# Two levels of Strassen for layer 0, and both layers of a two-layer graph network as streams of short pieces in a fixed order

## The chip, the core and the metric

The kernel runs on one core of a Trainium2 chip. The core has TensorE (PE in the profile: matrix products into PSUM; PEld is its weight load), VectorE (DVE), ScalarE (ACT), GpSimd (POOL) and SyncE (SP), which here only issues transfers; "SPq" in a row means the queue of SyncE. Sixteen DMA engines carry the transfers of all queues. The engines run beside each other and wait for each other by semaphores.

The metric is the time of one execution on the device in microseconds (us). The kernel before takes 2339.7 us (median of 3 runs, 2339.16 to 2340.62).

## The reference

There are 128 graphs ("batches") of 128 nodes with 512 features, all fp32. Layer 0 averages over neighbours; layer 1 diffuses with a transition matrix that it computes from its own scores.

```python
# layer 0
agg = einsum('bij,bjf->bif', adj, x) / max(sum(adj, -1), 1e-6)
x   = layernorm(x + relu(concat([x, agg], 2) @ W.T))
# layer 1, K = 3
Xw  = x @ Wv + bv
sj, si = Xw @ aw[:512, 0], Xw @ aw[512:, 0]
e   = leaky_relu(sj[:, None, :] + si[:, :, None] + ab, 0.2)     # a 128 x 128 matrix per batch
T   = adj * exp(e);  T = T / (sum(T, -1) + 1e-12)
H, Xk = 0, x
for k in range(3):
    H = H + Xk @ Wk[k] + bk[k]
    Xk = T @ Xk
out = layernorm(x + relu(H))
```

## The kernel before

The weight products use one level of Strassen: seven products instead of eight. Two batches make the block rows, the two halves of the 512 features the inner blocks, and the two weights of a layer the block columns. ScalarE and VectorE carry partial sums between PSUM banks while TensorE goes on.

```python
def fused_pair(name, lf, rf, mT):            # two batches, 14 matmuls of 512 columns, 2 aggregations
    X, Y, W, Z = (bank(f"{name}{n}") for n in "xywz")
    ...
    product(X, 1, lf, rf, True)
    nc.scalar.copy(Y, X)
    product(Z, 5, lf, rf, True)
    nc.scalar.copy(s5, Z)
    product(X, 6, lf, rf, False)
    nc.vector.tensor_add(W, X, s5)
    ...                                      # products 2, 7, 3 and 4 in the same manner
    nc.tensor.matmul(W, mT[0], u[:, 0], ...) # aggregation with the graph's matrix
    nc.tensor.matmul(Z, mT[1], u[:, 1], ...)
    return W, Z
```

The transition of a group (G = 4 batches, N = 128 nodes) gets its row of scores from TensorE. A transpose of one column, given as if it were 128 equal columns, leaves the row in all 128 partitions of a PSUM bank. Seven banks rotate among the products, and the eighth, of the pool `ps_t`, is for such uses:

```python
def transition(g):
    ...                                      # sc: scores of the group, si: those of the rows, with the constant
    pe = ps_t.tile([P, G, N], FP, name="pe", tag="tr")
    for b in range(G):
        nc.tensor.transpose(pe[:, b, :], sc[:, 0, b : b + 1].to_broadcast([P, P]), ident)
    T = p1.tile([P, G, N], FP, name="T")
    nc.vector.tensor_add(T, pe, si[:, :, None].to_broadcast([P, G, N]))
    nc.vector.scalar_tensor_tensor(T, T, SLOPE, T, ALU.mult, ALU.max)
    nc.scalar.activation(T, T, AF.Exp)
    ...                                      # times adj, rows normalised, blocks swapped by way of DRAM
```

The normalised output y of layer 0 goes to DRAM (`yd`) and comes back in blocks (`yb`), which VectorE transposes into the left factors of layer 1 (`yf`). A loop over pairs of batches calls the parts, with layer 1 three pairs behind:

```python
for t in range(len(steps) + 3):
    ...                                      # loads
    if t < len(steps):
        layer0(g, p)
        y_blocks(g, p)                       # y -> yd (issued by GpSimd), yd -> yb (issued by SyncE)
    ...
    if t >= 3:
        layer1(*steps[t - 3])
    if 1 <= t <= len(steps):
        y_factors(*steps[t - 1])
    if t < len(steps) and p == 1:
        transition(g)
```

Of the kernel before, what the change touches and what calls it, by code (L numbers as in the profile page):

```python
# [15 lines left out]
def kernel(  # L16
# [32 lines left out]

    nc = tc.nc  # L50
    P = 128
# [13 lines left out]
    p3 = ctx.enter_context(tc.tile_pool(name="p3", bufs=3))  # L65
    p5 = ctx.enter_context(tc.tile_pool(name="p5", bufs=5))
    dram = ctx.enter_context(tc.tile_pool(name="dram", bufs=3, space=bass.MemoryType.DRAM))
    small = ctx.enter_context(tc.tile_pool(name="small", bufs=4))
    ps_t = ctx.enter_context(tc.tile_pool(name="ps_t", bufs=1, space=bass.MemoryType.PSUM))
    ps_m = ctx.enter_context(tc.tile_pool(name="ps_m", bufs=7, space=bass.MemoryType.PSUM))  # L70

    def bank(name):
        return ps_m.tile([P, F], FP, name=name, tag="mm")
# [4 lines left out]
    xs, xbs, adjs = {}, {}, {}  # L78
# [8 lines left out]
    def load_x(g, p):  # L87
        b = g * G + 2 * p
        xs[g, p] = p3.tile([P, 2, F], FP, name="xg")
        nc.sync.dma_start(xs[g, p], x[b : b + 2].rearrange("b n f -> n b f"))  # L90

    def load_x_blocks(g, p):
        b = g * G + 2 * p
        xbs[g, p] = p2.tile([P, 2, Q, P], FP, name="xb")
        load_blocks(xbs[g, p], x[b : b + 2])

    def load_adj(g, eng=nc.sync):
        adjs[g] = p3.tile([P, G, N], FP, name="ag")
        eng.dma_start(adjs[g], adj[g * G : (g + 1) * G].rearrange("b i j -> i b j"))

    def load_weight(eng, dst, src, h):

        for q in range(Q):
            eng.dma_start(dst[q * R : (q + 1) * R, h * H : (h + 1) * H],
                          src[q * P + h * H * R : q * P + (h + 1) * H * R].rearrange("(c s) o -> s c o", s=R))


    w0_sb = const.tile([P, 2 * NC, F], FP)
    wk_sb = const.tile([P, K, NC, F], FP)
    wvt_sb = [p5.tile([P, H, F], FP, name=f"wvt{i}", tag="y") for i in range(2)]  # L110
# [4 lines left out]
    w2, w1 = w0_sb[:, NC:, :], w0_sb[:, :NC, :]  # L115
    load_weight(nc.scalar, w2, w0t[F:], 0)
    load_x_blocks(0, 0)
    load_weight(nc.scalar, w1, w0t[:F], 0)
    load_weight(nc.sync, w1, w0t[:F], 1)
    load_weight(nc.scalar, w2, w0t[F:], 1)  # L120
    load_adj(0)
    load_adj(1)
    load_x_blocks(0, 1)
    for i in range(2):
        nc.scalar.dma_start(wvt_sb[i], wvt[i * FH : (i + 1) * FH, :].rearrange("(c p) f -> p c f", p=P))
    load_x(0, 0)
    load_x_blocks(1, 0)

# [4 lines left out]
    ones = const.tile([P, P], FP)  # L133
# [5 lines left out]


    first = [bank(f"first{i}") for i in range(7)]
    for t in first:
        nc.tensor.matmul(t, ident, ident[:, None, :].to_broadcast([P, Q, P]), start=True, stop=True)
    for t in first:
        nc.tensor.matmul(t[:, :1], ident, ident[:, :1], start=False, stop=True, skip_group_check=True)

    def weight_sums(eng, name, b11, b12, b21, b22):

        t = const.tile([P, 3, H, b11.shape[2]], FP, name=name)
        t1, t2, t4 = t[:, 0], t[:, 1], t[:, 2]  # L150
        eng.tensor_sub(t1, b12, b11)
        eng.tensor_sub(t2, b22, t1)
        eng.tensor_sub(b12, b22, b12)
        eng.tensor_sub(t4, b21, t2)
        return [None, b11, b21, b22, t4, t1, t2, b12]

    f0 = weight_sums(nc.vector, "t0", w2[:, :H], w1[:, :H], w2[:, H:], w1[:, H:])


# [5 lines left out]
    def fold_constants():  # L165
        pb = ps_t.tile([P, F], FP, name="pb", tag="tr")
        nc.tensor.matmul(pb, ones[:K], bk_sb, start=True, stop=True)
        nc.scalar.copy(bias, pb)
        nc.vector.tensor_sub(bias[:, FH:], bias[:, FH:], bias[:, :FH])
# [5 lines left out]
        pc = ps_t.tile([P, F], FP, name="pc", tag="tr")  # L175
        nc.tensor.matmul(pc[:, :1], ones, t1, start=True, stop=True)
        nc.vector.tensor_add(cc, pc[:, :1], ab_sb)
        pw = ps_t.tile([P, F], FP, name="pw", tag="tr")
        for c in range(NC):
            nc.tensor.matmul(pw[:2], aw_sb[:, :, c], wvt_sb[c // H][:, c % H, :], start=(c == 0), stop=(c == NC - 1))  # L180
        w2row = p1.tile([2, F], FP, name="w2row", tag="scr")
        nc.scalar.copy(w2row, pw[:2])
        wm = small.tile([2, 1], FP, name="wm")
        nc.vector.tensor_reduce(wm, w2row, AX.X, ALU.add)
        nc.vector.tensor_scalar(wm, wm, 1.0 / F, None, ALU.mult)
        nc.vector.tensor_scalar(w2row, w2row, wm, None, ALU.subtract)
        for t in range(2):
            pr = ps_t.tile([P, F], FP, name="pr", tag="tr")
            nc.tensor.matmul(pr, ident[:2, t : t + 1].to_broadcast([2, P]), w2row, start=True, stop=True)  # L189
            nc.scalar.copy(wrow[:, t], pr)  # L190


    def left_factors(pool, name, src):

        t = pool.tile([P, 7, H, P], FP, name=name)
        a11, a12, a21, a22, s1, s2, s4 = (t[:, i] for i in range(7))
        for i in range(2):
            nc.vector.transpose(t[:, 2 * i : 2 * i + 2].rearrange("p a h (j r) -> p j (a h) r", r=R),  # L198
                                src[:, i].rearrange("p j (c s) -> p j c s", s=R))
        nc.vector.tensor_add(s1, a21, a22)  # L200
        nc.vector.tensor_sub(a21, a11, a21)
        nc.gpsimd.tensor_sub(s2, s1, a11)  # L202
        nc.gpsimd.tensor_sub(s4, a12, s2)
        return [None, a11, a12, s4, a22, s1, s2, a21]

    def product(dst, i, lf, rf, start):
        for c in range(H):
            nc.tensor.matmul(dst, lf[i][:, c, :], rf[i][:, c, :], start=(start and c == 0),  # L208
                             stop=(c == H - 1), skip_group_check=True)

    def fused_pair(name, lf, rf, mT):

        X, Y, W, Z = (bank(f"{name}{n}") for n in "xywz")
        s5 = p2.tile([P, F], FP, name="s5")
        u = p2.tile([P, 2, F], FP, name="u")
        product(X, 1, lf, rf, True)
        nc.scalar.copy(Y, X)
        product(Z, 5, lf, rf, True)
        nc.scalar.copy(s5, Z)
        product(X, 6, lf, rf, False)  # L220
        nc.vector.tensor_add(W, X, s5)  # L221
        product(Y, 2, lf, rf, False)
        nc.scalar.copy(u[:, 0], Y)
        product(X, 7, lf, rf, False)
        nc.vector.tensor_add(Z, X, s5)  # L225
        product(W, 3, lf, rf, False)
        product(X, 4, lf, rf, False)
        nc.scalar.copy(u[:, 1], X)
        nc.tensor.matmul(W, mT[0], u[:, 0], start=False, stop=True, skip_group_check=True)  # L229
        nc.tensor.matmul(Z, mT[1], u[:, 1], start=False, stop=True, skip_group_check=True)  # L230
        return W, Z

    def statistics(mv, t):
        st = small.tile([P, 6], FP, name="st")
        nc.vector.bn_stats(st, t)  # L235
        nc.vector.bn_aggr(mv, st)  # L236

    def layernorm(t, mv, rstd):

        ve = small.tile([P, 2], FP, name="ve")  # L240
        nc.gpsimd.tensor_scalar(ve, mv[:, :, 1], LN_EPS, None, ALU.add)  # L241
        nc.gpsimd.tensor_tensor(rstd, ve, nhalf, ALU.pow)  # L242
        for i in range(2):
            nc.gpsimd.tensor_scalar(t[:, i], t[:, i], mv[:, i, 0:1], rstd[:, i : i + 1], ALU.subtract, ALU.mult)  # L244

    def swap_blocks(name, src):

        d = dram.tile([G, P, N], FP, name=f"{name}d")
        nc.sync.dma_start(d.rearrange("b i j -> i b j"), src)
        t = p1.tile([P, G, Q, R], FP, name=f"{name}b")  # L250
        load_blocks(t, d)
        return t

    xfs, ans, aTs, ys, ybs, yfs, scs, Ts, TTs = {}, {}, {}, {}, {}, {}, {}, {}, {}

    def x_factors(g, p):
        xfs[g, p] = left_factors(p2, "xf", xbs.pop((g, p)))

    def degree_norm(g):
        deg = small.tile([P, G], FP, name="deg")  # L260
        nc.vector.tensor_reduce(deg, adjs[g], AX.X, ALU.add)
        nc.vector.tensor_scalar(deg, deg, DEG_EPS, None, ALU.max)
        rdeg = small.tile([P, G], FP, name="rdeg")
        nc.vector.reciprocal(rdeg, deg)
        an = p1.tile([P, G, N], FP, name="an")
        nc.vector.tensor_mul(an, adjs[g], rdeg[:, :, None].to_broadcast([P, G, N]))
        ans[g] = swap_blocks("an", an)

    def a_transpose(g):
        aTs[g] = p2.tile([P, G, N], FP, name="aT")  # L270
        nc.vector.transpose(aTs[g].rearrange("p g n -> p (g n)"), ans.pop(g).rearrange("p g j r -> p (g j r)"))

    def layer0(g, p):

        ys[g, p] = p5.tile([P, 2, F], FP, name="y")
        if p == 0:
            scs[g] = p2.tile([P, 3, G], FP, name="sc")
        hs = fused_pair("h", xfs.pop((g, p)), f0, [aTs[g][:, 2 * p + i, :] for i in range(2)])
# [152 lines left out]
```

## Time and profile before

| | value | where it is read |
|---|---|---|
| time | 2339.7 us | median of 3 runs |
| profiled span | 2335.1 us, mean granted clock 0.994 | the profile's head |

The main lines, and what they say of a group of four batches, are in the prediction below. This row of the table of instruction groups (line, engine, operation, output and inputs, shape, count; then busy us and mean ns; then the idle time of the engine before it and its releaser) is the broadcast of the scores:

```profile
L311 PE MATMUL pe<-ident,ss 128*128 128x128 f32 x128 | 19.7, 278 | 11.6 <-DVE ss L306 11.6
```

TensorE is busy with it for 19.7 us in the whole run. The 11.6 us of waiting are the start's gap of which the prediction speaks. This row of the list of transfers (output and input, queue, number of issues, size of each, and at the end the median us from issue to landing) is the way back of y:

```profile
yb<-yd SPq DMA_DIRECT2D x256, 128.0 KB, 2.8
```

### The profile page before, as it was taken

How to read it: one execution, taken by the hardware profiler on the slowest of the kernel's cores; microseconds unless marked ns; L12 is line 12 of the kernel's file. 1: busy time of each engine (PE TensorE's matmuls, PEld its weight loads, DVE VectorE, ACT ScalarE, POOL GpSimd, SP SyncE). 2: the span in 40 equal slices, each digit the busy share in tenths (PEclk: the TensorE clock that was granted, in tenths of full speed). 3: DMA queues.
4: the chain of work that ended last, by engine and by line, in shares of the span. 5: the costliest groups of instructions: out<-in, count | busy, mean ns of one | idle time of the engine just before them, and what ended most of it. 6: DMA issues, size and time to landing. Idle time of an engine off the chain costs nothing.

```text
span 2335.1 us, 19605 instructions
## 1 busy us (share of the span) xinstructions
PE 2303.7 (99%) x6316; PEld 1174.9 (50%) x6316; DVE 1263.3 (54%) x2732; ACT 435.8 (19%) x805; POOL 1030.3 (44%) x929
## 2 busy tenths in 40 slices
PE   9799999999999999999999999999999999999997
PEld 3355455455455455554554554555545545545554
DVE  5865555555654655654556555556545555554442
ACT  1111212112112112111121121121111111211211
POOL 3744444534534444435345344444353454454433
PEclk9899999999999999999999999999999999999999
DMA  9543332333323333333333333343233333332210
GB/s 211 136 127 86 106 91 84 92 88 104 94 83 95 95 86 111 86 86 92 88 102 94 85 93 95 86 113 94 78 90 93 97 94 85 94 93 63 63 45 27
DMA packets 363974, 217.33 MB, mean 93 GB/s; under 512 B 148573, under 2 KB 328797, under 8 KB 363872
## 3 DMA queue, kind: packets, MB, share of 16 engines
q1 hardware_dynamic: 342848, 143.19, 24.8%
q0 software_dynamic: 19520, 70.28, 8.2%
q10 hardware_dynamic: 1504, 2.62, 0.5%
q8 instruction: 49, 0.80, 0.1%
q14 instruction: 53, 0.43, 0.1%
HBM read 132.13 MB, written 83.89 MB: 93 GB/s over the span
## 4 chain that ended last, share of the span: by engine, by line
PE 97%; DVE 2%; DMA 1%; POOL 0%; issue 0%; POOLq 0%; ACTq 0%; DVEq 0%
PE vx L208 19%; PE hx L208 19%; PE o L208 16%; PE hw L208 5%; PE vw L208 5%; PE vy L208 5%; PE vz L208 5%; PE hz L208 4%; PE hy L208 4%; PE vz L230 3%; PE hz L230 2%; PE vw L229 2%; PE o L353 2%; PE o L355 2%; PE hw L229 2%; PE pe L311 1%
## 5 line engine op out<-in xcount | busy, mean ns | idle before, releaser
L202 POOL TENSOR_TENSOR yf<-yf 128x256 f32<-128x256 f32 x64 | 51.6, 806 | 906.3 <-DVE mv L236 894.2
L244 POOL TENSOR_SCALAR y<-y,mv,rstd 128x512 f32<-128x512 f32 x128 | 266.3, 2082 | 7.0
L244 POOL TENSOR_SCALAR y<-y,mv,sc 128x512 f32<-128x512 f32 x128 | 266.7, 2087 | 0.6 <-POOL sc L242 0.2
L208 PE MATMUL hx<-w_sb,xf 128*128 128x512 f32 x512 | 254.1, 599 | 2.9 <-DVE hw L221 2.8
L208 PE MATMUL vx<-wk_sb,yf 128*128 128x512 f32 x512 | 242.3, 594 | 0.9 <-DVE vw L221 0.9
L208 PE MATMUL hx<-t,xf 128*128 128x512 f32 x512 | 242.1, 595 | 1.2 <-issue 1.2
L208 PE MATMUL o<-wk_sb,yf 128*128 128x256 f32 x1024 | 242.2, 379 | 0.6 <-DVE o L348 0.6
L208 PE MATMUL vx<-t,yf 128*128 128x512 f32 x512 | 240.6, 592 | 0.0
L208 PEld LDWEIGHTS o<-wk_sb,yf 128*128 128x128 f32 x1024 | 192.1, 190 | 84.0 <-issue 37.8
L346 DVE TENSOR_TENSOR so<-o,bias 128x256 f32<-128x256 f32 x64 | 27.1, 424 | 367.6 <-PE o L208 367.6
L208 PE MATMUL o<-t,yf 128*128 128x256 f32 x768 | 206.9, 379 | 0.0
L208 PEld LDWEIGHTS o<-t,yf 128*128 128x128 f32 x768 | 145.9, 190 | 100.5 <-issue 68.4
L290 DVE SCALAR_TENSOR_TENSOR scr<-y,wrow 128x512 f32<-128x512 f32 x256 | 188.3, 736 | 1.6 <-PE pr L189 0.5
L198 DVE STREAM_TRANSPOSE xf<-xb 128x512 f32<-128x512 f32 x128 | 83.6, 691 | 163.6 <-PE hx L208 154.4
L241 POOL TENSOR_SCALAR ve<-mv 128x2 f32<-128x2 f32 x128 | 38.6, 302 | 299.2 <-DVE mv L236 299.2
L235 DVE BATCH_NORM_STATS2 st<-y 128x6 f32<-128x512 f32 x256 | 167.9, 675 | 2.4
L208 PEld LDWEIGHTS hx<-t,xf 128*128 128x128 f32 x512 | 97.2, 191 | 124.0 <-issue 124.0
L208 PEld LDWEIGHTS vx<-t,yf 128*128 128x128 f32 x512 | 97.3, 190 | 122.4 <-issue 122.0
L208 PEld LDWEIGHTS vx<-wk_sb,yf 128*128 128x128 f32 x512 | 97.3, 191 | 122.0 <-issue 112.2
L208 PEld LDWEIGHTS hx<-w_sb,xf 128*128 128x128 f32 x512 | 95.4, 192 | 75.1 <-issue 57.4
L359 DVE SCALAR_TENSOR_TENSOR y<-o,y 128x512 f32<-128x512 f32 x128 | 85.9, 671 | 71.3 <-PE o L353 71.1
L225 DVE TENSOR_TENSOR vz<-vx,s 128x512 f32<-128x512 f32 x64 | 44.7, 699 | 143.0 <-PE vx L208 142.9
(121 smaller groups left out, 3272.6 us busy)
## 6 DMA issues: line engine op xcount, KB each, us to landing
xb<-in_x_dram SPq DMA_DIRECT2D x256, 128.0 KB, 3.0
xg<-in_x_dram SPq DMA_DIRECT2D x64, 512.0 KB, 4.2
yd<-y POOLq DMA_DIRECT2D x64, 512.0 KB, 3.3
yb<-yd SPq DMA_DIRECT2D x256, 128.0 KB, 2.8
out_dram<-y POOLq DMA_DIRECT2D x64, 512.0 KB, 3.3
ag<-in_adj_dram SPq DMA_DIRECT2D x32, 256.0 KB, 2.8
and<-an SPq DMA_DIRECT2D x32, 256.0 KB, 2.3
anb<-and SPq DMA_DIRECT2D x128, 64.0 KB, 2.7
```

What stands on the lines that cost most here:

```text
L198: nc.vector.transpose(t[:, 2 * i : 2 * i + 2].rearrange("p a h (j r) -> p j (a h) r", r=R), src[:, i].rearrange("p j (c s) -> p j c s", s=R))
L202: nc.gpsimd.tensor_sub(s2, s1, a11)
L208: nc.tensor.matmul(dst, lf[i][:, c, :], rf[i][:, c, :], start=(start and c == 0), stop=(c == H - 1), skip_group_check=True)
L225: nc.vector.tensor_add(Z, X, s5)
L229: nc.tensor.matmul(W, mT[0], u[:, 0], start=False, stop=True, skip_group_check=True)
L230: nc.tensor.matmul(Z, mT[1], u[:, 1], start=False, stop=True, skip_group_check=True)
L235: nc.vector.bn_stats(st, t)
L244: nc.gpsimd.tensor_scalar(t[:, i], t[:, i], mv[:, i, 0:1], rstd[:, i : i + 1], ALU.subtract, ALU.mult)
L290: nc.vector.scalar_tensor_tensor(scr, ys[g, p][:, i, :], 1.0, wrow[:, t, :], ALU.mult, ALU.mult, accum_out=scs[g][:, t, b : b + 1])
L353: nc.tensor.matmul(Q0, tT[0], v1[:, 0], start=False, stop=True, skip_group_check=True)
L355: nc.tensor.matmul(Q1, tT[1], v1[:, 1], start=False, stop=True, skip_group_check=True)
L359: nc.vector.scalar_tensor_tensor(r, q, 0.0, r, ALU.max, ALU.add)
```

## The change

The change wants to save TensorE work. Layer 0's weight product takes two levels of Strassen over four batches: 7 × 7 = 49 products of 256 columns, in place of 2 × 14 of 512 columns. Both layers become generators of short pieces ("streams"). In step t one piece of layer 0 is followed by one of layer 1, which lags 24 steps; a group has 18 steps. All other work stands at numbered places in a table: place 2t comes between the two pieces of step t, and 2t + 1 after both. The order of instructions on every engine is exactly that of the program. The streams take all eight PSUM banks (`bA`, `bB`), every transfer of the steady part is issued by SyncE, and the scores are broadcast by way of DRAM. The diff, cut to its core:

```diff
-    ps_t = ctx.enter_context(tc.tile_pool(name="ps_t", bufs=1, space=bass.MemoryType.PSUM))
-    ps_m = ctx.enter_context(tc.tile_pool(name="ps_m", bufs=7, space=bass.MemoryType.PSUM))
+    psum = ctx.enter_context(tc.tile_pool(name="psum", bufs=1, space=bass.MemoryType.PSUM))
...
+    bA = [psum.tile([P, F], FP, name=f"bA{i}") for i in range(4)]
+    bB = [psum.tile([P, F], FP, name=f"bB{i}") for i in range(4)]
...
+    def outer_pair(i, j, evict):             # two of the seven outer products, side by side in a bank
+        def prod(bank, k, start=False):
+            for h, o in enumerate((i, j)):
+                mm(bA[bank][:, h * FH : (h + 1) * FH], left_of(o)[:, LEFT[k]], right_of(o)[:, RIGHT[k]], start and h == 0)
+        ...
+        prod(0, 6)
+        V.tensor_add(bA[2], bA[0], s5)       # "the L262 add" below
+        prod(1, 2)
+        yield
...
-        pe = ps_t.tile([P, G, N], FP, name="pe", tag="tr")
-        for b in range(G):
-            nc.tensor.transpose(pe[:, b, :], sc[:, 0, b : b + 1].to_broadcast([P, P]), ident)
+        d = dram.tile([G, N], FP, name="scd")
+        nc.sync.dma_start(d.rearrange("b n -> n b"), sc[:, 0, :])
+        Ts[g] = d, si
+
+    def t_load(g):
+        d, si = Ts[g]
+        T = p1.tile([P, G, N], FP, name="T", tag="aT")
+        da = d[:]
+        nc.sync.dma_start(T.rearrange("p g n -> p (g n)"), bass.AP(tensor=da.tensor, offset=da.offset, ap=[[0, P], [1, G * N]]))
...
+    PLACES = {                               # middle groups; the first and the last have tables of their own
+        ... (y_load, 1): 43, ... (t_scores,): 39, (t_load,): 42, (t_exp,): 45, ...
+        (y_turn, 1, 0): 45, (y_turn, 1, 1): 46, ...
...
+    with tc.manual_schedule(engines={ET.PE, ET.DVE, ET.Activation, ET.Pool, ET.SP}):
+        for t in range(NG * NA + LAG + 20):
+            next(a, None)
+            run([(f, *args) for f, args in beside.pop(2 * t, ())])
+            run(late)
+            if t >= LAG:
+                next(b, None)
+            run([(f, *args) for f, args in beside.pop(2 * t + 1, ())])
+            run(later)
```

Here `t_scores` makes the scores and issues their store, `t_load` issues the broadcasting load, `t_exp` adds the two scores and takes the exponential, `y_load` brings y back in blocks, and `y_turn` transposes those.

## The prediction

> **What bounds the kernel now.** I read the page first (busy shares, then the chain that ended last), then the table of stretches for three groups of four batches in the middle of the run, then TensorE's (PE's) timeline, and last the start, engine by engine.
>
> ```profile
> PE 2303.7 (99%) x6316; PEld 1174.9 (50%) x6316; DVE 1263.3 (54%) x2732; ACT 435.8 (19%) x805; POOL 1030.3 (44%) x929
> ...
> PE 97%; DVE 2%; DMA 1%; POOL 0%; issue 0%; POOLq 0%; ACTq 0%; DVEq 0%
> ```
>
> The chain is PE for 97% of the span. A busy PE alone would not prove a limit, because the ends of matmuls are modelled; the chain and the steps between starts do. The stretches, whose columns are length, then busy time of PE, weight loads, VectorE, ScalarE and GpSimd (instructions in brackets), clock, DMA share and GB/s:
>
> ```profile
> 936.00:1007.20 71.20, 71.20 (x198) 36.43 (x197) 38.83 (x85) 13.51 (x25) 31.41 (x28) 1.00 0.34 93
> 1007.20:1078.40 71.20, 71.20 (x198) 36.43 (x197) 38.81 (x85) 13.51 (x25) 31.41 (x28) 1.00 0.33 92
> ```
>
> A group takes 71.2 us, PE never idles and has its full clock, and no other engine passes 55%. The price of a matmul comes from its start-to-start steps in PE's timeline (start, us, then the group; two records make one fp32 matmul):
>
> ```profile
> 1013.14 1.88 PE L208 MATMUL hx<-t,xf 128*128 128x512 f32 x4
> 1014.85 1.88 PE L208 MATMUL hy<-w_sb,xf 128*128 128x512 f32 x4
> ...
> 1006.25 2.75 PE L208 MATMUL o<-wk_sb,yf 128*128 128x256 f32 x12
> 1008.84 1.02 PE L353 MATMUL o<-v,TT 128*128 128x512 f32 x2
> ```
>
> Two matmuls of 512 columns step 1.717 us, so one costs 0.858 us; six of 256 columns step 2.59 us, so one costs 0.432, just half. Columns set the price, and a narrow matmul pays nothing extra. One thing could break that: each matmul brings its own weights.
>
> ```profile
> L208 PEld LDWEIGHTS o<-wk_sb,yf 128*128 128x128 f32 x1024 | 192.1, 190 | 84.0 <-issue 37.8
> L290 DVE SCALAR_TENSOR_TENSOR scr<-y,wrow 128x512 f32<-128x512 f32 x256 | 188.3, 736 | 1.6 <-PE pr L189 0.5
> ```
>
> A load takes 190 ns, a record of 256 columns 216 ns, so it still hides. I use the second row for VectorE's bill below.
>
> **What the Trainium skill says.** "TensorE: Matmul & The Clock Gate", section "Step-by-step: what each phase is for", lets a next weight load run under the current matmul; the step of 0.432 us at 190 ns per load agrees. Its section "What's actually happening" has the clock fall after an idle window of about 3.4 us; here the 11.6 us gap at 74 us leaves a clock of 0.83 over 60 to 100 us, which fits. "SBUF — State Buffer", section "Who interferes with whom", says a VectorE instruction with two SBUF inputs and a GpSimd instruction that reads SBUF shut each other out, while one SBUF input is free of it. The trace agrees in part: a VectorE add of 256 columns at 70.69 us lasted 6.61 us (usually 0.39 to 0.50) while GpSimd made four tensor-tensor operations in a row; but scores at 47.55 us took their usual 0.69 us under a GpSimd normalisation, so I charge the lock to tensor-tensor alone.
>
> **The change, part by part.** (1) TensorE per group of four. Before: layer 0 has 2 pairs x (14 products + 2 aggregations) = 32 units of 512 columns; layer 1 has 2 x (14 + 2 + 7 + 2) = 50; together 82, or 70.4 us. Four broadcasting transposes add 0.45 us (a step of 35.84 against 35.39 us between pairs), and four aggregations that wait for ScalarE's copy step 0.94 instead of 0.86, adding 0.32. Sum 71.2, as measured. After: two levels of Strassen make 49 products of 256 columns = 24.5 units, with 4 aggregations 28.5; layer 1 keeps 50. So 78.5 units = 67.4 us. The transposes are replaced by a DMA broadcast, and a piece of the other layer now stands before an aggregation, so both extras go. Gain: 3.5 x 0.858 + 0.77 = 3.8 us per group, 121 us over 32 groups.
>
> (2) VectorE per group, counted in the new program order and priced from the rows of before: PSUM adds and residuals 21.9 (10 bank adds x 0.696, 22 of 256 x 0.43, 8 residuals x 0.67); statistics 8 x 0.84 = 6.7; scores 8 x (0.736 + 0.08) = 6.5; ten transposes x 0.69 = 6.9; inner sums 8 x 0.42 + 4 x 0.50 = 5.4; outer sums of 896, 896 and 1024 columns at 1.21 us per 1024 = 3.3; degree and transition 6.0. Sum 56.7 us of 67.4: 84%, from 55%. That is the largest new cost. It lies beside PE, but PE waits for those adds in a fixed order.
>
> (3) ScalarE: 13.5 plus smaller copies out of PSUM, about 19 us. GpSimd: 8 normalisations x 2.08 = 16.7, scales 4.7, y sums 3.1, four-wide sums (896, 896, 1024, 1024, 768 columns at 1.9 us per 1024) 8.6: 33 us, 49%, about as before, because its four DMA issues x 0.8 go to SyncE. Transfers stay near a third of DMA's capacity.
>
> (4) The ends. Before, the span less 32 x 71.2 is 57 us: 11 until useful products, constants, the waits up to 100 us, and 13 after the last matmul. After, layer 0 runs 24 pieces alone (32.6 us of PE). VectorE has about 63 us of work ordered before layer 1's first operands: weight sums 8 x 1.2 and 2 x 2.1, x sums, three groups of evictions (about 3.1 each), statistics and scores. It starts near 10 us, so layer 1 begins near 78 us, with 45 us lost by then. The transition's DMA round trips cost perhaps 6 more, layer 1 alone at the end about 3 (an add of 0.43 plus its signal is exposed in each pair), the tail 13: 67 or 68 us, some 11 worse than before.
>
> Sum of the profiled span: 2335 - 121 + 11 = 2225. I add 0.3 us of stall per group, 10 us, as my allowance for 84% VectorE in fixed order: 2235. Timed runs were 4.6 us above the profiled span, so 2240 us.
>
> **The rivals.** First, VectorE becomes the bound. For: 56.7 us, plus lock waits: GpSimd's tensor-tensor work of some 12 us per group covers 18% of it, and if six of VectorE's two-input operations each lost 1.2 us it would reach 64 of 67.4. Gaps of in-order waiting would then show on PE as 2 us or more per group: 2290 to 2310, hardly faster. Against: the adds PE waits for have one SBUF input, and the order puts the score and transition work mostly away from GpSimd's sums; pieces are arranged so that an add runs under other matmuls. Over a piece pair PE has 3.74 us and VectorE 3.15.
>
> Second, PE is never made to wait in the steady part and the start overlaps better than I think: then 2225 less perhaps 10 at the start, plus 4.6: about 2215 to 2220. For: tables of places that differ for the first, middle and last group look fitted with care. Against: the start's VectorE work is in one fixed list.
>
> Third, SyncE's single queue, which now carries all DMA issues in order, blocks behind a store that waits for a normalisation and delays the blocks of x. One delay of 3 us per group would make 2330, and nothing is gained. Against: landing takes 2 to 4 us in the rows of before, and loads are placed several pieces (3.7 us each) ahead of use.
>
> **Range and chances.** No stalls and a better start give the low end, about 2212. Two us of stall per group alone would give 2294; I end the range at 2285, as I hold the ordered lists to be mostly right. Within 2% begins at 2293, which needs the first or third rival nearly whole. Faster 0.91, same 0.08, slower 0.01.
>
> **What would show each step.** In the changed profile a middle group should last 67.4 to 68.5 us with PE above 98% and 256-column matmuls still stepping 0.43; larger steps would say weight loads no longer hide. VectorE should be 55 to 60 us per group; above 62 the lock is at work, and wide sums with long means would name it. The first layer-1 product should stand at 70 to 85 us; earlier or later corrects my start. If the chain shows VectorE or DMA above 8%, a rival has won. The prediction is wrong if the group takes over 69.5 us, or if the ends together cost much other than 68.

## More of the kernel before

Node j's score has to be added along the columns of a matrix whose rows are the nodes i. The kernel gets the scores as one number per partition (node). To use them as a row in every partition, it has to turn them and copy them to all partitions. Both kernels do this once for each group of four batches.

## The result, and the profile after

The changed kernel takes 2543.62 us (median of 4 runs, 2536.62 to 2548.06), beside 2339.43 us for the kernel before (4 runs, 2337.62 to 2340.62). The ratio is 1.0871, with a 95% interval of 1.0845 to 1.0897: slower by 8.7%, and 304 us above the prediction. Ratios here and below are the mean time of one kernel's runs over that of the other's of the same rounds, so they are not quite the ratio of the medians quoted.

The page of the kernel after, its first and fourth parts:

```profile
PE 2288.1 (90%) x7520; PEld 1465.9 (58%) x7520; DVE 1758.7 (69%) x3539; ACT 577.8 (23%) x1286; POOL 1198.1 (47%) x852
...
PE 53%; DVE 21%; DMA 20%; SPq 2%; issue 2%; POOL 1%; DVEq 0%; ACT 0%; POOLq 0%; ACTq 0%
```

PE is now idle for a tenth of the span, and the chain that ended last runs through DMA for a fifth of it, against 1% before. The mean granted clock is 0.947. The groups repeat as regularly as before: the multiplication that makes the scores starts at 84.5 us in the first group and at 2460.7 us in the last, so a group takes (2460.7 − 84.5) / 31 = **76.65 us** on average. The table of stretches (columns as in the prediction), for one middle group and two parts of it:

```profile
1020.00:1096.43 76.43, 69.73 (x232) 44.84 (x232) 53.49 (x108) 17.93 (x40) 35.76 (x25) 0.95 0.36 90
1076.60:1084.90 8.30, 8.30 (x41) 7.29 (x40) 4.76 (x10) 2.48 (x6) 4.55 (x2) 1.00 0.03 1
1084.90:1090.70 5.80, 4.21 (x16) 2.62 (x14) 0.00 (x0) 0.00 (x0) 0.00 (x0) 1.00 0.63 83
```

VectorE has 53.5 us of work in 76.4, so it is not the limit. The second line is odd: for 8.3 us the DMA engines move almost nothing (share 0.03, 1 GB/s). In the third, three engines do nothing at all. SyncE's timeline around those 8.3 us (start, us, then what it issued) says what was under way:

```profile
1076.62 0.36 SPq L451 DMA_DIRECT2D scd<-ss  x1
1084.93 0.33 SPq L459 DMA_DIRECT2D T<-scd  x1
1085.36 1.85 SPq L84 DMA_DIRECT2D yb<-yd  x4
```

The store of the scores is issued at 1076.62 us. The load that reads them back can be issued only when the store has landed, at 1084.9. The blocks of y stand behind that load in the queue, although they have nothing to do with it. Two more lines of the table of stretches divide the time in which the store is under way:

```profile
1077.00:1078.00 1.00, 1.00 (x7) 0.87 (x6) 1.00 (x3) 0.06 (x1) 1.00 (x1) 1.00 0.28 10
1078.00:1084.90 6.90, 6.90 (x34) 6.07 (x33) 3.39 (x8) 2.42 (x6) 3.15 (x2) 1.00 0.00 0
```

The DMA engines are busy within one microsecond (share 0.28); the packet records of the trace put 528 packets of 4 bytes between 1077.51 and 1077.95 us. Then they do nothing for 6.9 us (share 0.00), and only after that does the store count as landed.

VectorE, in its fixed order, takes up the story (square brackets: idle time before, and what ended it):

```profile
1083.98 0.43 DVE L541 TENSOR_TENSOR bB<-bB,os 128x256 f32<-128x256 f32 x1 [2.16 <-PE bB L245]
1090.73 0.69 DVE L465 TENSOR_TENSOR T<-T,si 128x512 f32<-128x512 f32 x1 [6.32 <-DMA T<-scd]
...
1094.30 0.71 DVE L238 STREAM_TRANSPOSE yf<-yb 128x512 f32<-128x512 f32 x1 [2.15 <-DMA yb<-yd]
1094.94 0.67 DVE L262 TENSOR_TENSOR bA<-bA,hs 128x512 f32<-128x512 f32 x1
```

VectorE waits 6.32 us for T, then 2.15 us for the blocks. Only then does it come to the L262 add, whose operands do not depend on either. PE needs that add:

```profile
1088.09 1.02 PE L245 MATMUL bB<-v,TT 128*128 128x512 f32 x2
1095.66 3.47 PE L245 MATMUL bA<-wf,xs 128*128 128x256 f32 x8 [6.54 <-DVE bA L262]
```

PE idles 6.54 us, and then eight records of 256 columns take 3.47 us, which elsewhere take 1.89. From 1095.66 to 1099.13 us the table of stretches gives a granted clock of 0.56. So PE pays once for the wait and once more for a lowered clock. The tables of the whole run, below, show that it is so throughout. The list of transfers, with the median us to landing at the end of each row:

```profile
yb<-yd SPq DMA_DIRECT2D x256, 128.0 KB, 3.3
...
T<-scd SPq DMA_DIRECT2D x32, 256.0 KB, 5.8
...
scd<-ss SPq DMA_DIRECT2D x32, 2.0 KB, 8.1
```

The smallest transfer of the steady part, 2 KB, takes longest to land. It writes "b n -> n b": 512 single numbers, each 4 bytes, one by one, to places of which two in succession are 512 bytes apart. The tables of waits of SyncE's queue and of PE (waiter, what it waited for: total us, times, longest):

```profile
SPq L459 <- DMA scd<-ss: 257.4, 32, 10.0
```

```profile
PE bA L245 <- DVE bA L262: 202.7, 61, 7.1
```

Two stretches of the chain that ended last (start, us, what) show both transfers as its links:

```profile
1076.62 8.29 DMA scd<-ss
1086.76 7.42 DMA yb<-yd
```

### The profile page after: what moved, and what is told of

Same layout as the page of the kernel before. It is cut to its first block, busy times and chain, and to the rows that moved or that the text cites. A ratio compares the mean times of both kernels' runs of the same rounds, so it can differ in the third digit from the quotient of the medians.

```text
span 2534.9 us, 23773 instructions
## 1 busy us (share of the span) xinstructions
PE 2288.1 (90%) x7520; PEld 1465.9 (58%) x7520; DVE 1758.7 (69%) x3539; ACT 577.8 (23%) x1286; POOL 1198.1 (47%) x852
## 4 chain that ended last, share of the span: by engine, by line
PE 53%; DVE 21%; DMA 20%; SPq 2%; issue 2%; POOL 1%; DVEq 0%; ACT 0%; POOLq 0%; ACTq 0%
PE bB L245 34%; PE bA L245 19%; DMA scd<-ss 11%; DVE scr L385 9%; DMA yb<-yd 8%; DVE st L368 3%; SPq L84 2%; DVE bA L262 2%; DVE y L334 2%; DVE bB L510 1%; DVE mv L369 1%; DVE bB L515 1%; DMA wf<-in_w0t_dram 1%; DVE xu L199 1%; DVE xu L197 1%
## 5 line engine op out<-in xcount | busy, mean ns | idle before, releaser
L245 PE MATMUL bB<-wk_sb,yf 128*128 128x512 f32 (+1 forms) x2048 | 741.1, 495 | 6.4 <-DVE yf L238 4.2
L245 PE MATMUL bB<-t,yf 128*128 128x512 f32 (+1 forms) x1536 | 560.7, 488 | 5.9 <-DVE yf L196 5.2
L245 PEld LDWEIGHTS bB<-wk_sb,yf 128*128 128x128 f32 x2048 | 398.5, 195 | 254.2 <-issue 206.3
L245 PE MATMUL bA<-wf,xs 128*128 128x256 f32 x896 | 268.9, 450 | 193.9 <-DVE bA L262 191.6
L245 PEld LDWEIGHTS bB<-t,yf 128*128 128x128 f32 x1536 | 292.5, 191 | 201.3 <-issue 166.4
L245 PE MATMUL bA<-wf,xu 128*128 128x256 f32 x1344 | 346.2, 390 | 22.4 <-DVE bA L262 11.1
L245 PEld LDWEIGHTS bA<-wf,xs 128*128 128x128 f32 x896 | 199.5, 227 | 269.7 <-DVE bA L262 217.8
L245 PEld LDWEIGHTS bA<-wf,xu 128*128 128x128 f32 x1344 | 253.4, 193 | 133.8 <-issue 46.6
L396 POOL TENSOR_SCALAR y<-y,mvo,rstd 128x512 f32<-128x512 f32 x128 | 265.4, 2080 | 7.0
L245 PE MATMUL bA<-wf,xl 128*128 128x256 f32 x896 | 214.5, 379 | 0.2 <-DVE bA L267 0.2
L262 DVE TENSOR_TENSOR bA<-bA,hs 128x512 f32<-128x512 f32 x96 | 65.6, 683 | 62.8 <-PE bA L245 62.8
```

Of the source, the lines that this page charges most:

```text
L245: nc.tensor.matmul(dst, lhsT, rhs, start=start, stop=True, skip_group_check=True)
L262: V.tensor_add(bA[2], bA[0], s5)
L396: S_.tensor_scalar(t, t, mv[:, 0:1], rstd, ALU.subtract, ALU.mult)
```

## The experiments

Theory: the 512-piece store of the scores is the whole cause. It lands late itself, and it holds up the transfers issued after it. VectorE's fixed order passes the delay on to PE, and the lowered clock adds to it. Rivals: VectorE's order alone (the add stands behind waits it does not need), VectorE's load or its exclusion by GpSimd, and the DMA round trip as such, whatever its form.

Each table line below is the median of 4 or 5 runs. "Group" is the average group by the same instruction as above.

| kernel | us | ratio to before | group, us |
|---|---|---|---|
| after | 2543.62 | 1.0871 | 76.65 |
| e1_pe_scores | 2276.54 | 0.9744 | 68.45 |
| e2_yload_first | 2507.57 | 1.0729 | 75.60 |
| e3_late_exp | 2421.71 | 1.0381 | 72.91 |
| e4_filler | 2483.66 | 1.0629 | 75.02 |
| e5_before_dram | 2679.81 | 1.1461 | |
| e6_idle_store | 2453.27 | 1.0487 | 73.95 |
| e7_act_queue | 2402.20 | 1.0274 | |
| e8_start_dve | 2276.70 | 0.9738 | |
| e9_row_store | 2275.56 | 0.9736 | 68.33 |
| e10_idle_store_16b | 2276.93 | 0.9742 | 68.45 |
| e11_idle_store_act | 2368.56 | 1.0134 | 71.24 |
| e12_idle_store_pool | 2283.35 | 0.9767 | 68.51 |

All results were correct. The kernel before took 2336.94 us in the rounds of e1 to e4, 2338.25 in those of e5 to e8, and 2336.58 in those of e9 to e12.

### e1: the scores broadcast by TensorE again

```diff
-        nc.sync.dma_start(d.rearrange("b n -> n b"), sc[:, 0, :])       # and the load of T
+        for b in range(G):                                              # at the place of the load
+            nc.tensor.transpose(bB[3][:, b * N : (b + 1) * N], sc[:, 0, b : b + 1].to_broadcast([P, P]), ident)
-        V.tensor_add(T, T, si[:, :, None].to_broadcast([P, G, N]))
+        V.tensor_add(T, bB[3].rearrange("p (g n) -> p g n", g=G), si[:, :, None].to_broadcast([P, G, N]))
```

At that place of the order bank `bB[3]` holds nothing that is still wanted, so no extra bank is needed.

> The changed kernel with one part undone: the scores go to all partitions by four TensorE transposes into a PSUM bank that is idle then, as in the kernel before, not by a store of 512 single elements and a broadcasting load through DRAM. VectorE and GpSimd keep all their work and their order. Theory 1 (the score's round trip of some 14 us holds SyncE's queue and VectorE's order, and TensorE waits behind them for one add per group): the wait of 6.5 us and the low clock after it go, the transposes cost 0.45 us, so a group falls from 76.4 to about 68 us and the time to 2250 to 2290 us. Rival 2 (VectorE is too full for a fixed order, 52 us in 76): its load is the same, so the group stays above 74 us and the time above 2470. Rival 3 (the narrow pieces themselves cost TensorE more): group above 70 us with no waits and larger steps per matmul.

Measured: 2276.54 us (2275.07 to 2277.82), ratio 0.9744 with an interval of 0.9729 to 0.9758. The change is worth 2.6% once this one part of it is undone. A middle group in the table of stretches, and the store of y in the list of transfers, for which e6 will show another value:

```profile
1011.28:1079.86 68.58, 68.42 (x239) 44.67 (x238) 53.39 (x110) 18.03 (x41) 36.65 (x26) 1.00 0.35 97
```

```profile
yd<-y SPq DMA_DIRECT2D x128, 256.0 KB, 2.7
```

PE is busy for 68.42 of 68.58 us at full clock, and VectorE has nearly the same work as in the kernel after, 53.39 us against 53.49. So the rival "VectorE's load or lock" falls for the steady part. This run does not yet tell the store from the round trip or from the order.

### e2 and e3: another order around the slow store

```diff
 e2, middle groups     -(y_load, 1): 43                      +(y_load, 1): 41
 e3, besides that      -(t_load,): 42  (t_exp,): 45  (t_sums,): 48  (t_norm,): 49
                       +(t_load,): 43  (t_exp,): 49  (t_sums,): 50  (t_norm,): 50
```

> The changed kernel with one place moved for the middle groups: SyncE issues the loads of the y blocks of one pair before the broadcasting load of the scores, so they no longer wait for the score store's landing. VectorE's order is left. If theory 1 holds with both waits (VectorE first for the scores, then for the y blocks), only the second of them goes: the scores still land near 14 us after they were made, the add that TensorE waits for comes some 1.5 us sooner, group about 75 us, time 2490 to 2510 us. If SyncE's queue alone were the cause, the whole wait goes: group 68, time about 2290. If neither matters: 2544.

> As e2_yload_first, and VectorE takes the scores (add, leaky part, then sums and scaling) four places later, behind the transposes of y and the adds that TensorE needs. The slow round trip through DRAM stays as it is. Theory 1 says that only the order makes it costly: no wait of over 2 us for that add, group 68 to 70 us, time 2270 to 2340 us. If the transfers themselves (512 packets of 4 bytes, a load from one row) disturb the other loads, or the later steps of the transition now come too late for the aggregation, a new wait appears and the time stays above 2400.

Measured: 2507.57 us for e2 and 2421.71 us for e3. In e2 the add of T is still placed early, and VectorE still waits 230.9 us for T in 31 groups. In e3, where that add comes late, the wait moves to the blocks of y. VectorE's timeline:

```profile
1045.81 0.71 DVE L238 STREAM_TRANSPOSE yf<-yb 128x512 f32<-128x512 f32 x1 [5.27 <-DMA yb<-yd]
```

The blocks were issued at 1033.24 us, just after the store, and took 10.7 us to land. The order therefore matters (e3 wins back 122 us of the 267 that separate the kernel after from e1), but it does not suffice. A transfer that is independent of the store, and no longer stands behind a wait for it, is late too.

### e4: useless work that keeps TensorE busy

```diff
+    def filler(g):                          # at place 47 of the 30 middle groups
+        for _ in range(7):
+            nc.tensor.matmul(bB[3], ident, ident[:, None, :].to_broadcast([P, Q, P]), start=True, stop=True)
```

> The changed kernel with useless work added: seven matmuls of 512 columns into an idle bank (6.0 us at full clock) in the middle groups, just where TensorE waits for the late add. Results stay right. If the wait of 6.5 us is where theory 1 says and the half clock after it costs what the trace shows (1.6 to 2.9 us per group), the group gets shorter, 76.4 to about 74.5, and the time 2470 to 2510 us. If the clock plays no part: 2544 within 10 us. If TensorE's wait is not there, or the time is limited by TensorE's work: up to 6 us more per group, about 2720.

Measured: 2483.66 us, 60 us less than the kernel after, with seven more matmuls in each of 30 groups. PE's timeline:

```profile
1070.78 6.17 PE L658 MATMUL bB<-ident 128*128 128x512 f32 x14
1076.79 1.89 PE L245 MATMUL bA<-wf,xs 128*128 128x256 f32 x8
```

The filler takes the place of most of the wait (PE still waits 38.3 us in all for the L262 add, against 202.7), and the records after it take 1.89 us instead of 3.47. The mean clock rises from 0.947 to 0.993. So the lowered clock costs about 60 / 30 = 2 us per group on top of the wait. The Trainium skill, "TensorE: Matmul & The Clock Gate", section "What's actually happening", lets full speed return after some 3.4 us of sustained work; 3.4 us at half speed would lose 1.7 us, an estimate from that page which agrees. This agrees with the bill of the kernel after: of its 8.20 us per group over e1, waits for the L262 add explain (202.7 − 9.8) / 32 = 6.0, where 9.8 us is the same wait in e1, and 2.2 us are left.

### e5: the same part alone in the kernel before

```diff
-            nc.tensor.transpose(pe[:, b, :], sc[:, 0, b : b + 1].to_broadcast([P, P]), ident)
+        nc.sync.dma_start(d.rearrange("b n -> n b"), sc[:, 0, :])
+        nc.sync.dma_start(T.rearrange("p g n -> p (g n)"), bass.AP(..., ap=[[0, P], [1, G * N]]))
```

> The kernel before with only the broadcast of the scores changed: store of 512 single elements and broadcasting load on SyncE's queue in place of the four TensorE transposes. One part of the change alone. If the round trip of some 14 us is harmful wherever SyncE and VectorE take things in a fixed order, VectorE waits near 10 us for the scores and TensorE for VectorE's next adds: some 5 us or more per group, time 2480 or above. If only the new kernel's short pieces make it harmful (here a pair step of 35 us lies between, and VectorE has 45% idle): 0.45 us per group less transposing, little waiting, time 2310 to 2350 us. The price of the part alone decides.

Measured: 2679.81 us, ratio 1.1461 (1.1445 to 1.1476). The part costs about 342 us in a kernel with neither Strassen's second level nor the fixed tables. Two rows from its waits of VectorE and of SyncE's queue:

```profile
DVE T L314 <- DMA T<-scd: 368.9, 32, 12.7
```

```profile
SPq L313 <- DMA scd<-ss: 343.2, 32, 11.2
```

The part is harmful by itself, even more so here, where nothing was arranged around it. That the kernel before might hide it, as the other branch of the expectation had it, was wrong.

### e6: a store for which nobody waits

```diff
 e1, and in t_scores:
+        d = dram.tile([G, N], FP, name="scd")
+        nc.sync.dma_start(d.rearrange("b n -> n b"), sc[:, 0, :])      # never read
```

> e1_pe_scores with the store of the 512 score elements put back, its result used by nobody: the transfer without its waits. If only the waits for the scores cost time (SyncE held, VectorE waiting): 2277 us within 10, and the y blocks still land in about 3 us. If the store's small packets keep the blocks of y behind them, as the landing time of 10.7 us in the run with the later exponentials suggests: y blocks land near 10 us, VectorE waits for them, TensorE for VectorE some 2 us and more per group, time 2330 to 2400 us.

Measured: 2453.27 us (2448.10 to 2454.89), above the 2330 to 2400 that I had expected even if the store held up others. A store whose result is never used costs 177 us of the 267. From its list of transfers, its timelines of SyncE and VectorE, and its PE timeline:

```profile
yd<-y SPq DMA_DIRECT2D x128, 256.0 KB, 12.6
...
scd<-ss SPq DMA_DIRECT2D x32, 2.0 KB, 10.2
```

```profile
1043.16 0.36 SPq L451 DMA_DIRECT2D scd<-ss  x1
1043.63 1.92 SPq L84 DMA_DIRECT2D yb<-yd  x4
...
1046.10 1.95 SPq L407 DMA_DIRECT2D yd<-y  x2
```

```profile
1058.20 0.71 DVE L238 STREAM_TRANSPOSE yf<-yb 128x512 f32<-128x512 f32 x1 [5.49 <-DMA yb<-yd]
```

```profile
1059.56 1.99 PE L245 MATMUL bA<-wf,xs 128*128 128x256 f32 x8 [3.46 <-DVE bA L262]
```

The four blocks of y issued right after the store, from 1043.63 us on, come so late that VectorE waits for them until 1058.20, and PE waits for the same L262 add as before. The two stores of y issued next, at 1046.10 us, are held as well: the median of all stores of y is 12.6 us here, against the 2.7 shown for e1. So the store hurts in two ways: by being waited for, and by holding up what is issued after it.

### e7 and e11: the store on ScalarE's queue

```diff
 e7: e3, e11: e6, each with
-        nc.sync.dma_start(d.rearrange("b n -> n b"), sc[:, 0, :])
+        nc.scalar.dma_start(d.rearrange("b n -> n b"), sc[:, 0, :])
```

> e3_late_exp with the score store issued from ScalarE's queue. If the blocks of y were late there because they stood behind the store's 512 packets in the same queue, they now go round them: landing near 3 to 4 us, no wait of VectorE for them, group 69 to 70 us, time 2290 to 2330 us. If it is the sixteen DMA engines that the small packets hold, whichever queue they come from: landing stays near 10 us and the time near 2420.

> As e6_idle_store, with the unused store issued from ScalarE's queue. If transfers behind it in SyncE's own queue were held only by the queue's order: y blocks land in 3 us again, time 2277 to 2300 us. If both queues share what the 512 pieces occupy: landing of the y blocks issued beside it stays at 8 to 12 us and the time within 40 us of 2453.

Measured: 2402.20 us for e7 (e3: 2421.71) and 2368.56 us for e11 (e6: 2453.27; e1: 2276.54). The time of e7 lies between its two branches, and so does that of e11. SyncE's transfers are still held: in e11 the blocks of y take up to 13.6 us to land, and VectorE waits 128.5 us for them, against 172.9 in e6. Their median landing of 2.9 us does not show it, because only one of the two pairs of a group is loaded near the store. By the landing times in the trace (medians of the 30 middle groups, as far as they are recorded), the first of the four blocks is issued 0.13 us before the store in e11 and lands in 4.0 us. In e6 it was issued 0.47 us after the store and took 12.5. The other three, issued after the store in e11 too, take 10.5 to 12.4 us. So a part of the gain can come from the order of issue; whether the queue itself helps is not separated from that.

### e12: the store on GpSimd's queue

The same edit as in e11, with `nc.gpsimd.dma_start`.

> As e6_idle_store, with the unused store issued from GpSimd's queue, which the profile lists as software dynamic. In the first 8 us after the store in the changed kernel the DMA engines were 3% busy, so the pieces seem to wait in front of the engines. If that is in what SyncE's and ScalarE's queues share and GpSimd's does not: y blocks land in 3 us, time 2277 to 2310 us (GpSimd has half its time free for the issue). If the engines or the memory hold the others up: landing near 10 us and time above 2400.

Measured: 2283.35 us (2282.13 to 2284.93), 7 us above e1. It looks as if GpSimd's queue spared the others, but the timelines of SyncE (two lines) and GpSimd give another reason. Under them stand the rows of the store and of the stores of y from the views of transfers:

```profile
1046.73 1.80 SPq L84 DMA_DIRECT2D yb<-yd  x4
...
1049.07 3.07 SPq L407 DMA_DIRECT2D yd<-y  x2
```

```profile
1048.81 0.85 POOL L451 DMA_DIRECT2D scd<-ss  x1
```

```profile
scd<-ss POOLq DMA_DIRECT2D x32, 2.0 KB, 12.4
```

```profile
DMA to landing us min/median/max: 2.0/2.9/13.7
```

The store itself still needs 12.4 us. But GpSimd, busy with a normalisation, comes to it only 2.1 us after the multiplication that makes the scores has begun (0.2 in e6; medians of the 30 middle groups), and by then the blocks of y are issued: they land in 2.5 to 3.0 us. The two stores of y near it, issued 0.3 and 3.0 us after it, take 11.6 and 10.4 us, as late as behind SyncE's store, while no store of y in e1 takes more than 6.8. Nothing waits for them long: PE's waits for the L262 add are 11.8 us in all, 9.8 in e1. So e12 does not show that GpSimd's queue holds others less. It shows that what is issued a little before the pieces is hardly held.

Nor do fewer packets help. The queue that the page calls software_dynamic has 128 packets in e1 and 1152 here, so 1024 / 32 = 32 packets a store. SyncE's queue has 380960 packets in e1, and in e6 this:

```profile
q1 hardware_dynamic: 397856, 214.57, 38.0%
```

That is (397856 − 380960) / 32 = 528 packets a store: one for each number, and 16 more. Yet the store with 32 packets lands no sooner, in 12.4 us against 10.2.

### e9: whole rows instead of single numbers

```diff
 after, with the scores turned once by TensorE; the load of T from DRAM stays, and the order of the rest
+        nc.tensor.transpose(bB[3][:G, :N], sc[:, 0, :], ident)         # place 41
+        L_.copy(scT, bB[3][:G, :N])
-        nc.sync.dma_start(d.rearrange("b n -> n b"), sc[:, 0, :])      # 512 pieces of 4 bytes
+        nc.sync.dma_start(d, scT)                                      # 4 pieces of 512 bytes
```

> The changed kernel with its round trip through DRAM and its order kept, only the store mended: one TensorE transpose makes four rows of 128 scores, ScalarE copies them, and SyncE stores 4 rows of 512 bytes in place of 512 single elements. If the small pieces of the store are the cause, it lands in 2 to 3 us (was 8 to 10), the broadcasting load follows early, the y blocks land in about 3 us, the group falls to 69 to 71 us and the time to 2280 to 2340 us. If a round trip through DRAM as such, or the broadcasting load of 256 KB from one row, is the trouble in this order: the wait stays over 3 us per group and the time above 2420.

Measured: 2275.56 us (2274.36 to 2277.66), ratio 0.9736 with an interval of 0.9722 to 0.9751. SyncE's timeline, to be read against that of the kernel after:

```profile
1043.66 0.28 SPq L458 DMA_DIRECT2D scd<-scT  x1
1044.85 0.33 SPq L466 DMA_DIRECT2D T<-scd  x1
1045.34 1.80 SPq L84 DMA_DIRECT2D yb<-yd  x4
```

The load follows the store after 1.19 us, where it took 8.31. The landing times of this run are not in its trace, but the load waits for the store. PE's waits for the L262 add fall from 202.7 to 11.9 us in all, and the time lies below the 2280 to 2340 us that I had expected. The round trip through DRAM, the broadcasting load, the single queue and the order of the other instructions are all still there, and the loss is gone. This run settles the cause: it is the form of the store, 512 single numbers.

### e10: pieces of 16 bytes

```diff
 e6 with the unused store laid out as the scores lie
-        nc.sync.dma_start(d.rearrange("b n -> n b"), sc[:, 0, :])
+        nc.sync.dma_start(d[:], sc[:, 0, :])                           # d is [N, G]: 128 pieces of 16 bytes
```

> As e6_idle_store (a store that nobody waits for), but laid out so that each partition's four scores go as one piece of 16 bytes: 128 pieces in place of 512, the same 2 KB. If the cost goes with the number of pieces: landing near 2.5 us (10.2 / 4), the stores and loads of y held up by some 2 us only, time 2277 to 2310 us. If a small write costs by itself, or by the 128 partitions: landing 6 us or more and time above 2380.

Measured: 2276.93 us, no different from e1 without any store. The row of its list of transfers:

```profile
scd<-ss SPq DMA_DIRECT2D x32, 2.0 KB, 1.4
```

The same 2 KB in a quarter of the pieces land in 1.4 us instead of 10.2, and sooner than the 2.5 us that I had expected from a cost in proportion to their number. SyncE's queue has (385568 − 380960) / 32 = 144 packets a store more than in e1, so the pieces are indeed 128, and 16 more. Their size (16 bytes for 4) and their places in DRAM (in a row, no longer apart) changed with their number, and no run separates the three.

### e8: the start

```diff
 e1, with weight sums of the start on VectorE
-        2: (5, 3, 4, S_) ... 4: (6, 2, 5, S_)          right_sums([V, S_, V, S_], f1)
+        2: (5, 3, 4, V) ...  4: (6, 2, 5, V)           right_sums([V, V, V, V], f1)
```

> e1_pe_scores with the start's weight sums that GpSimd did (two of 1792 columns for layer 0, two of 1024 for layer 1) put on VectorE: 4.0 plus 2.4 us more work for VectorE by its own rows, 13 us less of GpSimd tensor-tensor. In the start VectorE's operations with two SBUF inputs took up to 4.2 us instead of 0.7 while GpSimd did such sums. If that exclusion made layer 1 start at 93 us where my sum of VectorE's work said 78: it starts 4 to 10 us earlier, time 2266 to 2273 us. If VectorE's plain work is the limit: 6 us later, about 2283.

Measured in five rounds: 2276.70 us (2275.78 to 2278.95), and e1 had 2276.54. In e1's start, beside wide GpSimd sums, a VectorE product of two inputs with 512 columns had taken 4.20 us, where the median of the same line is 0.65, and one with 4 columns 3.92, so I had expected them to delay layer 1. Taking the GpSimd sums away gained nothing: layer 1's first product came at 96.76 us, against 93.44 in e1. What sets that start stays open.

## Why the prediction was wrong

**The step that failed** is in part (1): "The transposes are replaced by a DMA broadcast, and a piece of the other layer now stands before an aggregation, so both extras go." The saving was counted at 0.45 us per group, and the thing put in its place was never priced. No row of the profile before had a store of single numbers, and "landing takes 2 to 4 us in the rows of before" was read off transfers with other pieces; even there it holds for the steady part alone, as the rows of the start stand at 4.7 to 6.4 us. The store measured 8.1 us in the kernel after and up to 10 in its waits. e9, which changes the form of the store and turns the scores for it on TensorE, and e1, which removes the round trip, both give back the loss.

**The third rival was right in kind.** SyncE's queue did block behind a store and delay other blocks, but it was the store of the scores, not one that waits for a normalisation, and the blocks of y, not those of x. Its size was off: I gave it 3 us per group. Measured are 76.65 − 68.45 = 8.20 us: 6.0 of added waiting for the L262 add and 2.2 left, of which e4 shows about 2 to be the lowered clock. Over 32 groups that is 262 us, the difference of the two profiled spans (2534.9 − 2273.2).

**The sum of the miss.** The predicted span was 2235 us, the profiled one 2534.9. Groups: (76.65 − 67.7) × 32 = 286 us, where 67.7 is the predicted 67.4 plus the allowance of 0.3. Ends: 2534.9 − 32 × 76.65 = 82 us, predicted 67.5, so 15 us more. Together 301; the two spans differ by 300, as the parts of the prediction were rounded.

**TensorE's bill** was nearly right. In e1 a middle group has PE busy for 68.42 us, and the 256-column matmul still steps 0.43 us: in the kernel after, eight records start at 1084.64 us and the next at 1086.37, so 1.73 us for four matmuls. The average of 68.45 us is 1.0 above the 67.4 worked out. The four transposes are back in e1, at 0.45, and its waits for the L262 add are 9.8 / 32 = 0.3; the last 0.3 I did not trace. In e9, with one transpose of four columns in their place, the group still takes 68.33 us, so more may be missing than these three parts say. The gain over 71.20 is 2.75 us per group, against 3.8 predicted, 0.45 of which was the transposes.

**VectorE's bill** was 56.7 us and measured 53.5, GpSimd's 33 and measured 36, ScalarE's 19 and measured 18. One reading in it was too kind. The score multiplication at 47.55 us took its usual 0.69 us under a GpSimd normalisation, but the one before it, at 46.35 us under the same normalisation, took 1.16. In the kernel after, the 256 score multiplications average 899 ns, where 736 were charged; what slowed them was not tested. The first rival, VectorE as the bound, did not happen in the steady part: e1 has the same load and PE does not wait. But the chain of e1 still has VectorE at 21%, with PE busy for 98% of the span. So my sign "VectorE above 8% in the chain" does not tell a limit: the chain may pass through an engine that was merely the last to release a busy one. The DMA share did tell it: 20% in the kernel after, 1% in e1.

**The ends** were wrong by 15 us with or without the store (e1: 2273.2 − 32 × 68.45 = 83 us). Layer 1's first product was expected near 78 us and came at 94.91 in the kernel after and 93.44 in e1, which is about the size of the miss. That the one makes the other was not tested, and e8 ruled out the cause I had in mind.

**With the store mended**, the kernel would have fallen just inside the predicted range, 2275.56 of 2212 to 2285. The range ended where it did because I took "two us of stall per group" for the worst that the order could do, without asking what a single new transfer costs.

What stays open is why the store ends so late, and why it holds up what is issued after it. When I planned e12 I took the pieces to wait in front of the DMA engines. The packet records say otherwise: in the kernel after, the engines have recorded all 528 packets of a store 1.3 us after its issue, and it lands at 8.1 us (medians of 32 stores). The delay lies behind that, where no run looks.

## What to carry to other kernels

Price every new transfer by its contiguous pieces, their number and size, and not by its bytes alone: 512 pieces of 4 bytes took 8 to 10 us and held up what was issued after them, while the same 2 KB in 128 pieces of 16 bytes took 1.4 us. Where such a store cannot be avoided, issue first what is wanted soon; e12, where this came about by chance, lost only 7 us. Lay a small result out so that it can be stored in runs, or turn it on TensorE first, in a bank that is idle at that place of a fixed order. Where an engine has a fixed order, put the instruction that TensorE waits for ahead of any that waits for a DMA, since a late transfer is otherwise paid by TensorE, and a second time in its clock.

## What the Trainium skill lacked or had wrong

- "DMA: Bandwidth & Descriptors", section "Anatomy of one DMA — SWDGE (gpsimd) path", puts a transfer's fixed cost near 2.0 us and calls descriptor generation "small, variable", with many descriptors free before a cost shows, but not how many. Here 2 KB in 512 pieces landed in 12.4 us from GpSimd's queue. From SyncE's queue 512 pieces of 4 bytes took 8.1 to 10.2 us and 128 pieces of 16 bytes 1.4 us, so there the cost shows somewhere between the two.
- The same page, section "Rules for kernel authors", rightly says that a non-contiguous last dimension lowers to one descriptor per element and advises rearranging (528 packets per store agree). It does not warn that such a store delays the transfers issued after it: the 256 KB store of y went from 2.7 to 12.6 us. What the page says in its section "Queues, rings and completion order", that a completion signal waits for every earlier write of its DMA engine, may be a part of the reason; it gives no size, and no run here tests it.
